# A graph layer on one core: a small first block of dst, another order of additions and one-hots, banks shared out anew, and earlier x work

## The chip, the cores and the metric

The kernel runs on one core of one Trainium2 chip. The metric is the device time of one execution in microseconds; a median of several runs is compared.

TensorE multiplies and accumulates into PSUM, VectorE does elementwise work and reductions, ScalarE applies functions and copies, GpSimd clears memory and issues a few transfers, and the sync engine (SP) only issues transfers. Each engine takes its instructions in the order in which the program gives them to it.

## The reference

There are N = 12500 nodes with 128 features (x) and E = 412500 edges with 48 features. dst holds each edge's receiving node and is sorted. With one graph, whose 64 global numbers are u:

```python
h   = maximum(layernorm(x), 0)                          # [N, 128]
agg = segment_sum(edge_attr, dst, num_segments=N)       # [N, 48]
z   = relu(concat([h, agg, u]) @ W1 + b1)               # W1 [240, 256]
out = x + z @ W2 + b2                                   # W2 [256, 128]
```

All of it is float32.

## The kernel before, in words

**Sums over edges.** A chunk is 768 edges, 128 partitions with T = 6 edges each; there are 538 chunks. CG = 6 chunks make a group. The edges are swept in two halves at once, s = 0 and s = 1[...]: half 0 sums into partitions 0 to 47 of aggT, half 1 into 64 to 111. aggT is laid out with features on partitions and nodes along the free axis.

As dst is sorted, the edges of a chunk meet a window of 36 nodes. `onehot` (L296, VectorE) compares each edge's shifted dst (`rel`) with 0 to 35. `contract` (L306, TensorE) multiplies the edges (as weights) with these one-hots, six matmuls for a chunk of each half, into a PSUM bank of the group (`acc`). `add` (L322, VectorE) adds the 153 columns of a group's bank into aggT at an address that it reads from `lo_i`. There are NI = 45 groups in each half.

**Shifted dst.** dst comes in blocks of IB = 9 groups of both halves, 108 rows of 768 numbers. `shift_dst` (L345 to L348) makes the base of each row with a small matmul (`brow`, L328) and a ScalarE copy, and subtracts it on VectorE (`df`). `spread` (L361, L362) turns df with TensorE's transposes and copies it to `rel`, in two halves of three.

**The layer.** Nodes are taken in blocks of 512, four to a partition; a pair is one block from the lower and one from the upper half of the nodes, so that the two sweeps complete a pair together. There are 12 pairs and a middle block of 212 nodes. For a pair: `load_x` and `next_x` (L204, ScalarE's queue), `normalization` (statistics L432, variance, L418 to L422, and ReLU on ScalarE, L428), `transpose` (L444, copy L447), `hidden_x` (L462: x part of the first layer, one block and one half of the hidden units; with the first half also xb = x + b2, L458), `hidden_sums` (L473: sums part of both blocks, then ReLU to `hid`, L481), `output` (L492) and `store` (L500, L503). The x tiles have XBUFS = 3 buffers; xb is the last reader of one.

**The order.** It is written out by hand (`manual_schedule`). The main loop goes by steps of one chunk of each half. In each step it emits the contraction, then what stands at that step: at k = 0 and k = 3 of a group the one-hots of one half of the next group, followed by the addition of the group before; then stores that are due; then one part of the normalization (`next_part`); then `pieces` of the layer (transposes, hidden parts, outputs), each with a first step and a price, as far as a credit of 0.56 a step reaches. A pair's pieces become due when both sweeps have passed it (`ready`). A pair's statistics are followed by its ReLU rows, which wait in the list until the pair before has been transposed. As soon as both xb of a pair have been emitted, the load of the pair three further on is put into `x_loads`; `next_x` issues from it at every tenth step, or at once when the normalization gets to that pair. Edge loads go out on SP's queue, each after its buffer was read; PF = 15 buffers of two chunks. dst loads and stores of the output go on the same queue.

PSUM has eight banks here: three for group sums, one for transposes, two for the first layer, two for outputs.

Of the kernel before, what the change touches and what calls it, by code (L numbers as in the profile page):

```python
# [12 lines left out]
OP = mybir.AluOpType  # L13
# [8 lines left out]
def kernel(  # L22
# [50 lines left out]
    NG = -(-E // GE)  # L73
    NI = NG // 2
    IB = 9
    NB = NI // IB
    CB = IB * CG
    assert NG == 2 * NI and NI == NB * IB
# [6 lines left out]
    PF = 15  # L85
# [10 lines left out]
    for k in range(NP):  # L96
# [7 lines left out]
    HIGH = [END - OFF[-1] - W, N - 1]  # L104
    assert LOW[1] + OFF[0] + shift[1] == 0
    NC = max(HIGH[0] + WG, HIGH[1] - LOW[1] + WG, END + PAD + WA)


    ready = [min(NI - 1, max(
        int(-(-(blocks[j][0] + BN + PAD + 1 - LEAST - s * NI * GSTEP) // GSTEP)) - 1  # L110
# [7 lines left out]
    psh = ctx.enter_context(tc.tile_pool(name="ps_h", bufs=2, space=bass.MemoryType.PSUM))  # L118
# [7 lines left out]
    ohp = edge_ctx.enter_context(tc.tile_pool(name="oh", bufs=6))  # L126

    aggT = big.tile([P, NC], F32)
    brow = const.tile([1, NB, 2, IB, CG], F32)
# [8 lines left out]
    def load_edges(e, c0, n):  # L138
# [15 lines left out]
    chunks = [min(CG, NCH - g * CG) for g in range(NG)]  # L154
    edges, hots, rels = {}, {}, {}

    ends = [min(s * NI * CG + NI * CG, NCH) for s in range(2)]
    e_loads = sorted(
        (c - s * NI * CG, s, c, min(CL if c > NI * CG or s == 0 else 1, ends[s] - c))
        for s in range(2) for c in ([] if s == 0 else [NI * CG]) + list(range(s * NI * CG + s, ends[s], CL)))  # L160
# [9 lines left out]
    def load_chunks(di, at, c, n):  # L170

        full = max(0, min(n, NFULL - c))
        nc.sync.dma_start(di[at:at + full], dst[c * CE:(c + full) * CE].rearrange("(c e) -> c e", e=CE))
        if full < n:
            for q in range(0, CE, TAIL):
                m = min(TAIL, CE - q)
                nc.sync.dma_start(di[at + full:at + n, q:q + m], dst[None, E - m:E])

    rows_in = [CB + sum(chunks[NI + b * IB:NI + (b + 1) * IB]) for b in range(NB)]

    def load_dst(b):
        di = dp.tile([P, CE], I32, name="di", bufs=2)
        for s in range(2):
            g = s * NI + b * IB
            load_chunks(di, s * CB, g * CG, sum(chunks[g:g + IB]))
        return di
# [30 lines left out]
    mids = [min(g * GE + GE // 2, E - 1) for g in range(NG)]  # L217
    nf = min(sum(m == g * GE + GE // 2 for g, m in enumerate(mids)), E // GE)
# [8 lines left out]
    with nc.allow_non_contiguous_dma(reason="a few hundred numbers, once"):  # L227
        nc.sync.dma_start(first[:, :nf], dst[:nf * GE].rearrange("(a g e) -> a g e", a=1, e=GE)[:, :, GE // 2])
        for g in range(nf, NG):
            nc.sync.dma_start(first[:, g:g + 1], dst[None, mids[g]:mids[g] + 1])  # L230
        dis = {0: load_dst(0)}
        for i in range(PF):
            next_edges()
# [6 lines left out]
    for s in range(2):  # L240
        nc.gpsimd.memset(low[:, s * NI:(s + 1) * NI], float(LOW[s]))
        nc.gpsimd.memset(high[:, s * NI:(s + 1) * NI], float(HIGH[s]))
# [12 lines left out]
    cut = NC * 5 // 8  # L255
    for c in range(0, cut, 1024):
        nc.gpsimd.memset(aggT[:, c:min(c + 1024, cut)], 0.0)
# [4 lines left out]
    nc.gpsimd.iota(least, pattern=[[1, NG]], base=0, channel_multiplier=0,  # L262
# [18 lines left out]
    for i in range(3):  # L281
        ps = psum.tile([P, 512], F32, name=f"ps{i}")
        nc.scalar.copy(ps, zero.to_broadcast([P, 512]))
        acc.append(ps)
    nc.scalar.copy(aggT[:, cut:], zero.to_broadcast([P, NC - cut]))


    def onehot(s, i, k0=0, k1=CG):
        if i < NI:
            g = s * NI + i  # L290
            n = min(k1, chunks[g]) - k0
            if k0 == 0:
                hots[g] = ohp.tile([P, CG * T, W], F32, name="oh")
            c = s * CB + i % IB * CG + k0
            r = rels[i // IB][:, c:c + n, :].rearrange("p c t -> p (c t)")
# [3 lines left out]
    def contract(i, k):  # L299
# [3 lines left out]
        groups = [(s, s * NI + i) for s in range(2) if k < chunks[s * NI + i]]  # L303
        for t in range(T):
            for s, g in groups:
                nc.tensor.matmul(  # L306
                    ps[s * HI:s * HI + DE, o:o + W], edges[g * CG + k][0][:, t * DE:(t + 1) * DE],
                    hots[g][:, k * T + t, :], start=(k == 0 and t == 0),
                    stop=(k == chunks[g] - 1 and t == T - 1), skip_group_check=True)
        for s, g in groups:  # L310
            if edges.pop(g * CG + k)[1]:
                next_edges()

    def add(s, i):
# [3 lines left out]
            lo_i[0:1, g:g + 1], engines=[DVE], min_val=0, max_val=HIGH[s] - LOW[s],  # L318
# [6 lines left out]
    def first_nodes():  # L325

        for s in range(2):
            nc.vector.tensor_tensor(  # L328
                brow[:, :, s].rearrange("a b i k -> a b (i k)").rearrange("a b (i k) -> a b i k", k=CG),
                offs[:, None, None, :].to_broadcast([1, NB, IB, CG]),  # L330
                first[:, s * NI:(s + 1) * NI].rearrange("a (b i) -> a b i", i=IB)[:, :, :, None]
                .to_broadcast([1, NB, IB, CG]), OP.add)
# [8 lines left out]
    def shift_dst(b, di):  # L341
# [3 lines left out]
        nc.tensor.matmul(pb[:rows], brow[:, b].rearrange("a s i k -> a (s i k)")[:, :rows], one, start=True, stop=True)  # L345
# [5 lines left out]
    def spread(b, df, rows, parts=(0, 1), start=False):  # L351

        dv = df.rearrange("c (p t) -> c t p", t=T)
        if 0 in parts:
            rels[b] = dp.tile([P, P, T], F32, name="rel", bufs=2)
        q = T // 2
        for t0 in [a * q for a in parts]:
            own = start and t0
            pt = (psh if own else pst).tile([P, q, P], F32, name="ph" if own else "pt")
            for t in range(q):  # L360
                nc.tensor.transpose(pt[:, t, :rows], dv[:rows, t0 + t, :], ident[:rows, :rows])  # L361
            (nc.vector.tensor_copy if own else nc.scalar.copy)(  # L362
                rels[b][:, :rows, t0:t0 + q].rearrange("p c t -> p t c"), pt[:, :, :rows])
# [9 lines left out]
    def decide():  # L373
# [4 lines left out]
        nc.vector.tensor_scalar(least, least, GSTEP, float(LEAST), OP.mult, OP.add)  # L378
# [60 lines left out]
    def transpose(j):  # L439
# [6 lines left out]
        hT = mp.tile([P, P, R], F32, name="hT", bufs=3)  # L446
# [5 lines left out]
    def hidden_x(k, a, j):  # L452
# [7 lines left out]
        phs[j] = psh.tile([P, BN], F32, name="ph")  # L460
        for c in (0, HI):
            nc.tensor.matmul(phs[j][c:c + HI, :R * m], w1h[:, a * P + c:a * P + c + HI], hTs[j][:, :R * m],  # L462
                             start=True, stop=False, skip_group_check=True)

    def hidden_sums(k, a):

        js = pairs[k]
        if len(js) == 2:
            for s, j in enumerate(js):
                at = blocks[j][0] + shift[s]  # L470
                h = slice(s * HI, s * HI + DE)
                for c in (0, HI):
                    nc.tensor.matmul(phs[j][c:c + HI], w1a[h, a * P + c:a * P + c + HI], aggT[h, at:at + BN],  # L473
                                     start=False, stop=True, skip_group_check=True)
        else:
            for c in (0, HI):
                nc.tensor.matmul(phs[js[0]][c:c + HI, :NM], w1a[:K2, a * P + c:a * P + c + HI], mid[:K2],
                                 start=False, stop=True, skip_group_check=True)
        for j in js:
            m = blocks[j][1]  # L480
            nc.scalar.activation(hids[j][:, a, :, :m], phs.pop(j)[:, :R * m].rearrange("h (p r) -> h r p", r=R),  # L481
# [35 lines left out]
    pieces = [(18, 0.9, lambda: turn(0)), (20, 0.9, lambda: turn(1))]  # L517
    for k, js in enumerate(pairs):
        at = CG * ((ready + [NI - 1])[k] + 1) + 4
        nxt = pairs[k + 1] if k + 1 < len(pairs) else []  # L520
        if len(js) == 1:
            pieces.append((at, 0.0, lambda: copy_middle(0)))
        for a in range(NH):
            for j in js:
                pieces.append((at - 2, 0.9, lambda k=k, a=a, j=j: hidden_x(k, a, j)))
            pieces.append((at, 0.9, lambda k=k, a=a: hidden_sums(k, a)))
# [12 lines left out]
    def next_part(force=False):  # L539

        nonlocal begun
        if not parts and begun < len(pairs):
# [30 lines left out]
    first_nodes()  # L573
    dfs = {0: shift_dst(0, dis[0])}
    spread(0, dfs[0], rows_in[0], start=True)
    for k0 in (0, CG // 2):
        for s in range(2):
            onehot(s, 0, k0, k0 + CG // 2)
    first_columns()
    next_x()  # L580
    next_x()

# [151 lines left out]
```

## Time and profile before

| | |
|---|---|
| runs | 362.89, 357.94, 361.99 us; median 361.99 |
| profiled execution | 365.58 us; its span 363.5 |
| mean TensorE clock in it | 0.946 |
| TensorE busy | 315.6 us (87%), 7785 instructions |
| VectorE busy | 230.0 us (63%) |
| ScalarE busy | 110.6 us (30%) |
| moved | 95.37 MB, 262 GB/s over the span |
| edge matmuls, L306 | 195.0 us busy, 25.3 us idle before them |
| one-hots, L296 | 134.1 us busy, 1461 ns of one |

The span runs from the first to the last instruction. A busy time is the sum of an engine's instructions; for TensorE their ends are modelled. "Idle before" is how long the engine stood still ahead of instructions of that group, and the name behind it is what ended the wait; "issue" means that the profile shows nothing that it waited for. The clock is the share of full speed that TensorE was granted. The first edge matmul starts at 10.91 us and the last ones end near 327.5 us; the last instruction of TensorE ends at 356.4 us.

### The profile page before, as it was taken

The page shows a single profiled execution, that of the slowest core. Times are in us where ns is not written, and L with a number is a line of the kernel's source. Part 1 is how long each engine was busy: PE and PEld are TensorE (multiplying, and loading weights), DVE is VectorE, ACT ScalarE, POOL GpSimd, SP SyncE. Part 2 cuts the span into 40 slices and gives each one's busy share as a digit, 9 for nine tenths or more (in the row PEclk, how much of TensorE's full clock was granted, in tenths as well). Part 3 has the DMA queues.
Part 4 walks back from the last instruction along what each step waited for, and adds up shares of the span by engine and source line. Part 5 has one row for each costly group of instructions (what it writes and reads, how often), then busy time and mean ns, then how long its engine had stood idle before and what let it go on. Part 6 is the DMA issues. An engine that isn't in the chain of part 4 may idle for free.

```text
span 363.5 us, 17319 instructions
## 1 busy us (share of the span) xinstructions
PE 315.6 (87%) x7785; PEld 252.4 (69%) x7786; DVE 230.0 (63%) x445; ACT 110.6 (30%) x231; POOL 10.8 (3%) x40
## 2 busy tenths in 40 slices
PE   1788599999969989988999998999899979998781
PEld 1777576866956877766886885886696766884271
DVE  1877698577566577756578587569458566833220
ACT  6105042325212341521251263033243241243230
POOL 9200000000000000000000000000000000000000
PEclk9969989999998999999899999699899998999987
DMA  6999999999996999999799949999889997510101
GB/s 178 334 334 347 359 359 330 307 324 345 307 286 189 309 303 289 318 313 301 207 304 316 300 136 351 358 303 326 273 271 313 299 320 221 163 62 2 58 35 46
DMA packets 81233, 95.37 MB, mean 262 GB/s; under 512 B 5484, under 2 KB 74234, under 8 KB 81149
## 3 DMA queue, kind: packets, MB, share of 16 engines
q1 hardware_dynamic: 77331, 87.27, 76.0%
q10 hardware_dynamic: 3530, 6.40, 5.2%
q8 instruction: 63, 1.03, 1.2%
q0 software_dynamic: 288, 0.49, 0.5%
q14 instruction: 21, 0.17, 0.1%
HBM read 87.75 MB, written 6.40 MB: 259 GB/s over the span
## 4 chain that ended last, share of the span: by engine, by line
PE 80%; DMA 6%; issue 6%; DVE 4%; ACT 1%; SPq 1%; DVEq 0%; ACTq 0%
PE ps L306 42%; PE po L492 13%; PE ph L462 11%; PE ph L473 7%; PE pt L444 4%; DMA e<-in_edge_attr_dram 3%; DVE oh L296 2%; DMA xt<-in_x_dram 2%; PE pt L361 1%; DMA di<-in_dst_dram 1%; ACT hid L481 1%; DVE aggT L322 0%; ACT xn L428 0%; DVE df L348 0%; DVE xb L458 0%
## 5 line engine op out<-in xcount | busy, mean ns | idle before, releaser
L306 PEld LDWEIGHTS ps<-oh,e 128*48 128x48 f32 x6456 | 186.0, 131 | 75.2 <-issue 68.3
L306 PE MATMUL ps<-oh,e 128*48 128x36 f32 x6456 | 195.0, 218 | 25.3 <-issue 21.7
L296 DVE TENSOR_TENSOR oh<-iota,rel 128x1296 f32<-128x1296 f32 (+1 forms) x92 | 134.1, 1461 | 0.3
L481 ACT ACTIVATE hid<-ph,bias 128x512 f32<-128x512 f32 (+1 forms) x50 | 31.3, 675 | 127.1 <-PE ph L473 121.4
L492 PE MATMUL po<-w,hid 128*64 128x128 f32 (+1 forms) x784 | 64.6, 290 | 0.2 <-ACT hid L481 0.2
L462 PE MATMUL ph<-hT,w1h 128*64 128x512 f32 (+1 forms) x200 | 52.9, 606 | 1.5 <-ACT hid L481 1.5
L322 DVE TENSOR_TENSOR aggT<-aggT,ps 48x153 f32 x90 | 28.0, 311 | 40.4 <-PE ps L306 28.2
L500 DVE TENSOR_TENSOR ot<-po,xb 128x512 f32<-128x512 f32 (+1 forms) x25 | 17.3, 691 | 50.4 <-PE po L492 50.1
L492 PEld LDWEIGHTS po<-w,hid 128*64 128x64 f32 (+1 forms) x784 | 45.7, 144 | 1.2 <-ACT hid L481 0.8
L428 ACT ACTIVATE xn<-xt,sh,sc 128x128 f32<-128x128 f32 (+1 forms) x100 | 40.5, 483 | 3.1 <-DVE sh L422 2.3
L447 ACT COPY hT<-pt 128x512 f32<-128x512 f32 (+1 forms) x25 | 14.4, 576 | 55.3 <-PE pt L444 54.9
L473 PE MATMUL ph<-aggT,w1a 48*64 48x512 f32 x192 | 27.3, 631 | 4.1 <-DVE aggT L322 4.1
L432 DVE BATCH_NORM_STATS2 st<-xt 128x6 f32<-128x128 f32 (+1 forms) x100 | 23.6, 279 | 8.7 <-DMA xt<-in_x_dram 8.3
L444 PE MATMUL pt<-ident,xn 128*128 128x128 f32 (+1 forms) x100 | 17.9, 298 | 2.3 <-ACT xn L428 1.7
L458 DVE TENSOR_TENSOR xb<-xt,b_sb 128x512 f32<-128x512 f32 (+1 forms) x25 | 16.8, 683 | 0.2
L444 PEld LDWEIGHTS pt<-ident,xn 128*128 128x128 f32 (+1 forms) x100 | 11.2, 146 | 5.8 <-ACT xn L428 3.6
L462 PEld LDWEIGHTS ph<-hT,w1h 128*64 128x64 f32 x200 | 11.4, 140 | 5.4 <-ACT hid L481 4.1
L362 ACT COPY rel<-pt 128x324 f32<-128x324 f32 (+1 forms) x9 | 6.8, 754 | 23.4 <-PE pt L361 21.4
L348 DVE TENSOR_TENSOR df<-di,base 108x768 f32<-108x768 int32 (+1 forms) x5 | 4.8, 955 | 13.3 <-ACT base L346 6.7
L370 ACT ACTIVATE far<-df,bounds 108x768 f32<-108x768 f32 (+1 forms) x10 | 9.4, 936 | 7.4 <-DMA e<-in_edge_attr_dram 7.3
L473 PEld LDWEIGHTS ph<-aggT,w1a 48*64 48x64 f32 x192 | 5.2, 131 | 7.9 <-DVE aggT L322 4.5
L146 POOL MEMSET e<- 128x288 f32 x1 | 0.3, 343 | 299.9 <-PE ps L306 299.9
(74 smaller groups left out, 63.8 us busy)
## 6 DMA issues: line engine op xcount, KB each, us to landing
e<-in_edge_attr_dram SPq DMA_DIRECT2D x268, 288.0 KB
xt<-in_x_dram ACTq DMA_DIRECT2D x24, 256.0 KB
out_dram<-ot SPq DMA_DIRECT2D x24, 256.0 KB
di<-in_dst_dram SPq DMA_DIRECT2D x9, 162.0 KB
di<-in_dst_dram SPq DMA_DIRECT2D x1, 153.0 KB
e<-in_edge_attr_dram SPq DMA_DIRECT2D x1, 144.0 KB
di<-in_dst_dram SPq DMA_DIRECT2D x9, 0.3 KB
w1h<-in_L_gnn_W_dram POOLq DMA_DIRECT2D x1, 128.0 KB, 6.6
```

The costliest lines, as they stand in the source:

```text
L296: nc.vector.tensor_tensor(hots[g][:, k0 * T:(k0 + n) * T], iota[:, None, :].to_broadcast([P, n * T, W]), r[:, :, None].to_broadcast([P, n ...
L306: nc.tensor.matmul(ps[s * HI:s * HI + DE, o:o + W], edges[g * CG + k][0][:, t * DE:(t + 1) * DE], hots[g][:, k * T + t, :], start=(k == 0 ...
L322: nc.vector.tensor_tensor(to, to, acc[i % len(acc)][h, :wg], OP.add)
L428: nc.scalar.activation(xns[j][:m, r], xs[j][:m, r], AF.Relu, bias=sh[:m, c:c + 1], scale=sc[:m, c:c + 1])
L432: parts.append((k, None, lambda i=i, j=j, r=r: nc.vector.bn_stats(st[:m, i * R + r, :], xs[j][:m, r, :])))
L444: nc.tensor.transpose(pt[:, r, :m], xn[:m, r], ident[:m, :m])
L458: nc.vector.tensor_tensor(xb[:m], xs[j][:m], b2_sb[:m, None, :].to_broadcast([m, R, D]), OP.add)
L462: nc.tensor.matmul(phs[j][c:c + HI, :R * m], w1h[:, a * P + c:a * P + c + HI], hTs[j][:, :R * m], start=True, stop=False, skip_group_check ...
L473: nc.tensor.matmul(phs[j][c:c + HI], w1a[h, a * P + c:a * P + c + HI], aggT[h, at:at + BN], start=False, stop=True, skip_group_check=True)
L481: nc.scalar.activation(hids[j][:, a, :, :m], phs.pop(j)[:, :R * m].rearrange("h (p r) -> h r p", r=R), AF.Relu, bias=bias[:, a:a + 1])
L492: nc.tensor.matmul(pos[j][c:k, r], hids[j][:, a, r, c:k], w2[:, a], start=(a == 0), stop=(a == NH - 1), skip_group_check=True)
L500: nc.vector.tensor_tensor(ot[:m], pos.pop(j)[:m], xbs.pop(j)[:m], OP.add)
```

## The change

- **Blocks of dst.** Blocks begin at groups 0, 2, 11, 20, 29 and 38, so the first holds two groups of each half (24 rows). The halves are split at chunk 269 (`C0`), so the last group of both halves is short. The first block's dst goes on ScalarE's queue and the second's on SP's behind the seventh edge load. `rel` is one tile for each half, so `spread` copies twice.
- **VectorE's order.** Both additions of the group before stand at k = 0, ahead of the next group's one-hots; one-hots of half 0 follow at k = 0, of half 1 at k = 2. One-hot tiles have two buffers for each half instead of six in all. The very first one-hots come in thirds.
- **PSUM.** Three banks for the first layer, two for group sums.
- **Layer.** The first two pairs are transposed from steps 8, 11, 14 and 17. Later, pairs are transposed two ahead instead of one (hT has four buffers), x parts are due eight steps before the sums instead of two, and one x part of the second half stands ahead of the first sums. Parts of the normalization come two in a step in the first 20 steps and in odd steps later; a pair is begun only when its x buffer can have been freed. Credit is 0.54 a step, up to 1.2. `next_x` stands at steps 4, 7, 12 and then every eighth.
- **Others.** PF is 18. GpSimd clears all of aggT. The loop ends three steps after the last contraction.

```diff
-    PF = 15
+    PF = 18
...
-    psh = ctx.enter_context(tc.tile_pool(name="ps_h", bufs=2, space=bass.MemoryType.PSUM))
+    psh = ctx.enter_context(tc.tile_pool(name="ps_h", bufs=3, space=bass.MemoryType.PSUM))
...
-    ohp = edge_ctx.enter_context(tc.tile_pool(name="oh", bufs=6))
+    ohp = edge_ctx.enter_context(tc.tile_pool(name="oh", bufs=2))
...
-    for i in range(3):
+    for i in range(2):
         ps = psum.tile([P, 512], F32, name=f"ps{i}")
...
-    pieces = [(18, 0.9, lambda: turn(0)), (20, 0.9, lambda: turn(1))]
+    order = [j for js in pairs for j in js]
+    pieces = [(8 + 3 * j, 0.9, lambda j=j: turn(j)) for j in order[:4]]
     for k, js in enumerate(pairs):
-        at = CG * ((ready + [NI - 1])[k] + 1) + 4
-        nxt = pairs[k + 1] if k + 1 < len(pairs) else []
+        at = CG * ((ready + [NI - 1])[k] + 1) + 2
+        nxt = pairs[k + 2] if k + 2 < len(pairs) else []
...
-        for a in range(NH):
-            for j in js:
-                pieces.append((at - 2, 0.9, lambda k=k, a=a, j=j: hidden_x(k, a, j)))
-            pieces.append((at, 0.9, lambda k=k, a=a: hidden_sums(k, a)))
+        parts_of = [(at - 8, 0.9, lambda k=k, a=a, j=j: hidden_x(k, a, j)) for a in range(NH) for j in js]
+        sums = [(at, 0.9, lambda k=k, a=a: hidden_sums(k, a)) for a in range(NH)]
+        m = len(js)
+        pieces += parts_of[:m + 1] + sums[:1] + parts_of[m + 1:] + sums[1:]
...
-        if not parts and begun < len(pairs):
+        if not parts and begun < min(len(pairs), freed + XBUFS):
             normalization(begun)
...
+    for step in [4, 7] + list(range(12, CG * NI, 8)):
+        at_step(0, step, next_x)
...
-        if k in (0, 3):
-            onehot(k // 3, i + 1)
-            if 0 <= i - 1 < NI:
-                add(k // 3, i - 1)
+        if k == 0:
+            if i > 0:
+                add(0, i - 1)
+                add(1, i - 1)
+        if k == 0:
+            onehot(0, i + 1)
+        if k == 2:
+            onehot(1, i + 1)
         store_late()
-        if step >= 4:
+        for _ in range(2 if step % 2 or step < 20 else 1):
             next_part()
-        if step >= 14 and step % 10 == 4:
-            next_x()
-        credit = min(credit + 0.56, 1.0)
+        credit = min(credit + 0.54, 1.2)
```

## The prediction

> **What bounds the kernel now.** I read the page's summary first, then the chain, the waits of the sync engine's DMA queue by stretch, and the order of time where TensorE stops.
>
> ```profile
> span 363.5 us, 17319 instructions
> PE 315.6 (87%) x7785; PEld 252.4 (69%) x7786; DVE 230.0 (63%) x445; ACT 110.6 (30%) x231; POOL 10.8 (3%) x40
> PE 80%; DMA 6%; issue 6%; DVE 4%; ACT 1%; SPq 1%; DVEq 0%; ACTq 0%
> ```
>
> TensorE is the bound: 80% of the chain. The DMA engines look full, but the sync queue waits for landings only early. The waits of 30 to 60 us (first line) and of 60 to 100 us (the other two; us, times, longest):
>
> ```profile
> SPq L142 <- DMA e<-in_edge_attr_dram: 10.6, 17, 2.7
> ...
> SPq L142 <- PE ps L306: 16.9, 23, 1.7
> SPq L142 <- DMA e<-in_edge_attr_dram: 2.5, 2, 1.7
> ```
>
> From 60 us edge loads wait for buffers that TensorE frees, so a TensorE stall is lost time. It also costs twice, as pairs of stretches show, a gap and what follows (stretch, its us, busy us of TensorE, weight loads, VectorE, ScalarE, GpSimd, then TensorE's clock, DMA share, GB/s):
>
> ```profile
> 19.00:20.60 1.60, 0.05 (x3) 0.02 (x2) 0.00 (x0) 0.00 (x0) 0.00 (x0) 1.00 1.09 368
> 20.60:27.00 6.40, 6.36 (x129) 6.13 (x131) 6.34 (x14) 0.00 (x0) 0.00 (x0) 0.50 1.08 330
> 107.00:109.10 2.10, 0.05 (x2) 0.00 (x0) 2.07 (x4) 0.00 (x0) 0.00 (x0) 1.00 1.05 343
> 109.10:114.00 4.90, 4.85 (x74) 2.70 (x76) 4.40 (x9) 1.27 (x2) 0.00 (x0) 0.65 0.40 122
> 226.20:227.80 1.60, 0.04 (x1) 0.00 (x0) 0.19 (x2) 0.56 (x2) 0.00 (x0) 1.00 1.08 372
> 227.80:236.00 8.20, 8.19 (x142) 7.88 (x143) 4.50 (x7) 0.74 (x2) 0.00 (x0) 0.58 1.09 357
> ```
>
> These gaps are followed by clocks of 0.50, 0.65, 0.58: 3.2, 1.7, 3.4 us lost. Of ten gaps of 1.4 us or more seven had such a sequel, about 2 us each; three had none.
>
> VectorE's order is the other thing to see. In time order:
>
> ```profile
> 13.28 3.23 ACTq L204 DMA_DIRECT2D xt<-in_x_dram  x2
> 20.61 0.49 DVE L432 BATCH_NORM_STATS2 st<-xt 128x6 f32<-128x128 f32 x2 [3.54 <-DMA xt<-in_x_dram]
> 21.02 1.49 DVE L296 TENSOR_TENSOR oh<-iota,rel 128x1296 f32<-128x1296 f32 x1
> ...
> 109.15 1.84 PE L473 MATMUL ph<-aggT,w1a 48*64 48x512 f32 x8 [2.10 <-DVE aggT L322]
> 345.92 1.42 PE L444 MATMUL pt<-ident,xn 53*128 53x53 f32 x4 [1.73 <-ACT xn L428]
> ```
>
> Statistics that wait for x hold back the one-hots queued behind them (3.54 us). TensorE at L473 waits for VectorE's latest addition into aggT. The last line is a stall of the tail.
>
> **What the Trainium skill says.** "TensorE: Matmul & The Clock Gate", Part 1: the default clock is half speed, and idle windows of about 3.4 us bring it back. The trace agrees on the half (0.50), but gaps of 1.6 us were enough. "DMA: Bandwidth & Descriptors", Anatomy of one DMA: about 2.0 us fixed plus bytes over 436 GB/s (a software-queue fit), an estimate of 2.6 us for 256 KB. The chain of waits has one x load from 181.45 to 184.23, 2.78 us; in the saturated start one took 5.52. I use 2.8. "Perfetto Trace Analysis", Per-engine timelines: VectorE's queue is strictly first in, first out; the lines at 20.61 and 21.02 agree.
>
> **Part by part.** Durations: one step of edge matmuls 0.58 us (48 loads in 1.16), hidden_x 0.95, hidden_sums 1.02, one-hots 1.5, an addition 0.32, xb 0.65, statistics 0.25.
>
> *Start.* Edge matmuls run steadily from 11.66. The small block drops the 2.21 us clearing of aggT from ScalarE's path, shrinks brow (2 of 0.42) and the rel copies (0.72; 36 columns instead of 324), and one-hots come in thirds (1.5 times 432/1296, 0.5). df stays 0.96 (768 columns for 24 rows too). From the landing of first at 3.4: brow 0.3, matmul and copy to base (ScalarE is free near 4.7) 1.0, df 0.96 and its 0.1 of waits, transposes 0.8, rel 0.5, two one-hot thirds 1.0: a start near 8.5, a gain of 3. It is given back: statistics of pair 0, then df of block 1, stand ahead of the one-hots of group 1, and x still lands near 15. Following both queues, group 1 starts near 18.5, group 2 near 27 (24.8 before), group 4 near 42.3; at 42.3 the old kernel is 5.5 steps further (3.2 us), but the new one has done 2.8 us of transposes ahead. Net 0, from -3 to +4. The new dst loads keep their bytes; block 1's load on SP holds eleven edge loads for 0.33 MB, 1 us, in a full queue. GpSimd's longer clearing (seven instructions for four of 0.95 us) starts its weight loads 2.5 us later; step 10 is their first user, hidden; otherwise at most 2.5. The split rel copies (two for one of 0.75) lie in ScalarE's 70% of idle time; up to 0.5 per half block, ten of them, if not. Ten tiny loads at the tail of dst held SP for 8.1 us near 206 and still do, earlier by 10 steps; three more edge buffers hide them, else 1.6 (the gap at 226.2).
>
> *Additions first, two banks, two one-hot buffers.* hidden_sums no longer finds additions behind one-hots: the waits of 2.1 and 1.6 us (near 109 and 172) go, with their slow clocks (4.9 and 4.8 us at 0.65, 1.7 each): -7. Next late is VectorE: additions 0.65 and two one-hots 3.0 fit into a group's 3.5 us of edge matmuls only barely, with hidden_x (2.85) easily. Behind the addition's wait for the previous group stand both one-hots of the next.
>
> *Statistics now run to the limit of the x buffers.* This is the costly part. Before, next_x ran 5 to 15 steps ahead of a pair's statistics. Now parts run a pair further ahead with XBUFS still 3, so pair k+3's load is issued just after the last xb of pair k frees its buffer, and its statistics stand next on VectorE, ahead of additions. For k=2, from the end of group 11: additions 0.65, one-hots 1.5, xb 0.65, one-hots 1.5, xb 0.65: 4.95. Load 2.8, its second half 0.75 later: 8.5; statistics and additions 1.1: 9.6. TensorE needs six steps and three hidden_x, 6.35, then three steps, 1.75: at 8.1 it stands at hidden_sums, which reads aggT: a stall of 1.5. Pair 6 (k=3): df of block 3 stands between the one-hots, after TensorE's base matmul at 2.7, so xb ends at 6.2, additions at 10.8; sums come one step into the next group, at 7.2: 3.6. Pair 7 (k=4): the second one-hots stand behind two statistics, 2.8 + 2.8 + 0.5 + 1.5 = 7.7 against 6.4 of TensorE, and once more a group later, 0.9: 2.2. Pair 3 starts with VectorE late (one-hots of group 4 at 42.3): 3.0. Pairs 4, 8, 9, 10, 11, 12 by their own orders: 1.4, 1.3, 2.0, 2.2, 2.0, 3.0. With 1.5 for pair 5 the ten sum to 22 us. Ten gaps times 0.7 times 2 us of slow clock add 14. Some old "issue" gaps (1.4 to 2.7 us, in mid-step) will hide in these: -5. Net +31; from 0 (landings within 1.3 us) to 58 (5.5 us, ten times 2.7 more).
>
> *Tail.* From 327.5 to 356.4 TensorE does two pairs and the middle. Now one pair and the middle remain: four hidden_x 3.8, two sums 2.0, two waits for hid 1.6 (0.8 each, as at 329.76), outputs 5.1, middle 4.0: 16.5. Moved into the loop: two hidden_x, two sums, three transposes (0.6), 32 output matmuls (3.95): 9.7. Net 28.9 - 16.5 - 9.7 = -2.7; with three banks and the last transposes early, between -5 and 0.
>
> Sum: 0 - 7 + 31 - 2.7 = +21.3 on the profiled execution's 365.6, 387. That execution is 1% above the median of the runs, 361.99; with the difference carried over: 383.
>
> **Rivals.** *The wait is absorbed* (faster). VectorE is idle 37% of the time; if x lands soon enough that additions are done when TensorE reaches hidden_sums (point of decision: 1.3 us after issue, or TensorE later by that much), only -7 and -2.7 stay, and -3 of the start: 349 to 352. For it: VectorE is 2 to 4 us ahead of TensorE in many places. Against: 2.78 measured, and load issue hangs on VectorE itself. *The stalls replace the old ones* (no change): the mid-loop issue gaps, some 13 us with 8 of slow clock, vanish while TensorE waits elsewhere: 383 - 21 = 362. *Saturated landings* (worse): 5.5 us instead of 2.8: 383 + 27 = 410; against it, edge loads stop queueing at 60 us. That x parts come early may also do nothing: credit, not their due step, mostly sets them; that is within the tail's bounds.
>
> **How the numbers follow.** Forecast 0.58, worse 0.05, no change 0.13, faster 0.24. The forecast's own range is 371 to 396 (clock sequels between none and all, the start's bounds). To leave out at most 2 in 10, the range goes down to 351, halfway into the faster case, and up to 396. About 2% is what a measurement of this kernel tells from no change. Slower 0.62, same 0.14, faster 0.24.
>
> **What would show it.** Waits of VectorE's statistics for x of 2 to 4 us, ten times; waits of TensorE's sums and edge matmuls for VectorE of 15 to 25 us in all; a mean clock below 0.946; first edge matmul before 9.5; TensorE's work after the last edge matmul near 17 us. I'm wrong if statistics hardly wait for x, or if TensorE's waits for VectorE stay below 8 us.

## The result and the profile after

The changed kernel takes 422.8 us (median of 4 runs, 421.2 to 426.1), the kernel before 362.4 us in the same comparison: a ratio of 1.173 with a 95% interval of 1.159 to 1.186. The direction was forecast, the size was not: 383 us was predicted, and 396 us was the upper end of the range. The profiled execution took 426.1 us, its span is 424.1 us.

Lines have moved in the changed kernel: contract is L321, onehot L311, add L337, statistics L459, hidden_x L489 (xb L485), hidden_sums L500, output L519, df L366, the copies to rel L379 and L380, the x load L211.

The page's summary and the first line of its chain, kernel after:

```profile
span 424.1 us, 17390 instructions
PE 339.3 (80%) x7793; PEld 263.1 (62%) x7794; DVE 234.0 (55%) x460; ACT 111.1 (26%) x247; POOL 13.0 (3%) x44
PE 54%; DMA 18%; DVE 18%; issue 4%; ACT 2%; DVEq 1%; SPq 1%; ACTq 0%
```

TensorE has fallen from 80% of the chain to 54%; DMA and VectorE have 18% each. Two sums say where the 60.6 us of span went. TensorE's idle time (span less busy time) rose from 363.5 - 315.6 = 47.9 to 424.1 - 339.3 = 84.8 us: 36.9 us. Its busy time rose by 23.7 us for nearly the same instructions (7785 before, 7793 now). That second part goes with the clock, whose mean fell from 0.946 to 0.878.

The waits of the engines, kernel after (us in total, times, longest):

```profile
DVE st L459 <- DMA xt<-in_x_dram: 68.1, 14, 7.2
PE ph L500 <- DVE aggT L337: 34.1, 8, 6.5
PE ps L321 <- DVE oh L311: 12.7, 5, 5.5
PE ph L500 <- issue: 7.1, 1, 7.1
PE ps L321 <- issue: 3.6, 8, 0.8
```

VectorE's statistics wait for x for 68.1 us; before it was 8.3 us in 3 waits. TensorE's sums wait 34.1 us for additions, its edge matmuls 12.7 us for one-hots; before, 4.1 and 3.2. The edge matmuls' issue gaps have shrunk from 21.7 to 3.6 us.

One of the ten waits in time order, kernel after (start, duration, engine, line, what; in brackets the idle time before it and what ended it):

```profile
123.77 0.68 DVE L485 TENSOR_TENSOR xb<-xt,b_sb 128x512 f32<-128x512 f32 x1
...
124.46 2.32 PE L321 MATMUL ps<-oh,e 128*48 128x36 f32 x96
...
124.48 0.82 ACTq L211 DMA_DIRECT2D xt<-in_x_dram  x2
129.88 1.29 DVE L459 BATCH_NORM_STATS2 st<-xt 128x6 f32<-128x128 f32 x5 [5.43 <-DMA xt<-in_x_dram]
131.48 0.31 DVE L337 TENSOR_TENSOR aggT<-aggT,ps 48x153 f32 x1 [0.31 <-DVE st L459]
...
131.84 2.54 PE L500 MATMUL ph<-aggT,w1a 48*64 48x512 f32 x8 [5.06 <-DVE aggT L337]
...
134.31 2.14 PE L321 MATMUL ps<-oh,e 128*48 128x36 f32 x48
```

The last xb of a pair frees the x buffer, ScalarE issues both loads at once, and the next instruction of VectorE needs them. The additions stand behind the statistics, and TensorE, done with its edge matmuls at 126.78, stands at the sums until 131.84.

The same place in stretches, kernel after (stretch, its us, busy us of TensorE, weight loads, VectorE, ScalarE, GpSimd, then TensorE's clock, DMA share, GB/s):

```profile
127.00:129.00 2.00, 0.00 (x0) 0.00 (x0) 0.00 (x0) 0.00 (x0) 0.00 (x0) 1.00 1.07 370
129.20:131.80 2.60, 0.00 (x0) 0.00 (x0) 1.48 (x6) 0.00 (x0) 0.00 (x0) 0.59 1.08 360
131.80:146.00 14.20, 13.24 (x168) 8.15 (x168) 8.23 (x17) 2.72 (x5) 0.00 (x0) 0.50 0.52 152
146.50:150.00 3.50, 3.50 (x110) 3.50 (x108) 0.30 (x1) 2.44 (x5) 0.00 (x0) 0.97 0.77 208
```

The clock falls while TensorE is still idle, and stays at half for 14 us after it has resumed: half of 13.2 busy us, 6.6, are lost after a gap of 5. After the gaps of 1.6 us shown of the kernel before it was 3.2 to 3.4.

### The profile page after: what moved, and what is told of

It reads as the page before. It is cut to its first block, busy times and chain, and to the rows that moved or that the text cites. A ratio compares the mean times of both kernels' runs of the same rounds, so it can differ in the third digit from the quotient of the medians.

```text
span 424.1 us, 17390 instructions
## 1 busy us (share of the span) xinstructions
PE 339.3 (80%) x7793; PEld 263.1 (62%) x7794; DVE 234.0 (55%) x460; ACT 111.1 (26%) x247; POOL 13.0 (3%) x44
## 4 chain that ended last, share of the span: by engine, by line
PE 54%; DMA 18%; DVE 18%; issue 4%; ACT 2%; DVEq 1%; SPq 1%; ACTq 0%
PE ps L321 26%; DMA xt<-in_x_dram 13%; PE po L519 11%; DVE oh L311 9%; PE ph L500 7%; PE ph L489 6%; DMA e<-in_edge_attr_dram 5%; PE pt L471 4%; DVE xb L485 2%; DVE aggT L337 2%; DVE st L459 2%; ACT xn L455 1%; ACT hid L508 1%; PE pt L387 1%; DVE ot L527 1%
## 5 line engine op out<-in xcount | busy, mean ns | idle before, releaser
L321 PEld LDWEIGHTS ps<-oh,e 128*48 128x48 f32 x6456 | 191.0, 137 | 78.2 <-issue 63.9
L321 PE MATMUL ps<-oh,e 128*48 128x36 f32 x6456 | 197.7, 223 | 16.5 <-DVE oh L311 12.7
L311 DVE TENSOR_TENSOR oh<-iota,rel 128x1296 f32<-128x1296 f32 (+2 forms) x94 | 133.8, 1440 | 4.7 <-ACT rel L379 3.5
L500 PE MATMUL ph<-aggT,w1a 48*64 48x512 f32 x192 | 38.6, 772 | 41.2 <-DVE aggT L337 34.1
L337 DVE TENSOR_TENSOR aggT<-aggT,ps 48x153 f32 (+1 forms) x90 | 28.0, 311 | 75.9 <-PE ps L321 61.5
L489 PE MATMUL ph<-hT,w1h 128*64 128x512 f32 (+1 forms) x200 | 60.7, 686 | 1.9 <-ACT hid L508 1.9
L459 DVE BATCH_NORM_STATS2 st<-xt 128x6 f32<-128x128 f32 (+1 forms) x100 | 22.6, 280 | 68.2 <-DMA xt<-in_x_dram 68.1
L519 PE MATMUL po<-w,hid 128*64 128x128 f32 (+1 forms) x784 | 57.7, 278 | 0.7 <-ACT hid L508 0.7
L519 PEld LDWEIGHTS po<-w,hid 128*64 128x64 f32 (+1 forms) x784 | 42.5, 137 | 2.6 <-ACT hid L508 1.4
L500 PEld LDWEIGHTS ph<-aggT,w1a 48*64 48x64 f32 x192 | 8.4, 154 | 47.2 <-DVE aggT L337 37.5
L474 ACT COPY hT<-pt 128x512 f32<-128x512 f32 (+1 forms) x25 | 14.4, 575 | 47.1 <-PE pt L471 47.1
L445 ACT ACTIVATE sc<-va,eps 128x8 f32<-128x8 f32 (+1 forms) x13 | 3.9, 301 | 84.5 <-DVE va L444 81.2
L471 PE MATMUL pt<-ident,xn 128*128 128x128 f32 (+1 forms) x100 | 18.8, 314 | 4.4 <-ACT xn L455 3.4
L485 DVE TENSOR_TENSOR xb<-xt,b_sb 128x512 f32<-128x512 f32 (+1 forms) x25 | 16.8, 683 | 0.0
L489 PEld LDWEIGHTS ph<-hT,w1h 128*64 128x64 f32 x200 | 12.6, 154 | 4.6 <-ACT hid L508 3.2
L387 PE MATMUL pt<-ident,df 108*128 108x108 f32 (+2 forms) x33 | 7.6, 347 | 8.2 <-DVE df L366 8.2
L379 ACT COPY rel<-pt 128x162 f32<-128x162 f32 (+2 forms) x11 | 4.6, 415 | 29.7 <-PE pt L387 29.7
```

The source lines that it names most:

```text
L311: nc.vector.tensor_tensor(hots[g][:, k0 * T:(k0 + n) * T], iota[:, None, :].to_broadcast([P, n * T, W]), r[:, :, None].to_broadcast([P, n ...
L321: nc.tensor.matmul(ps[s * HI:s * HI + DE, o:o + W], edges[c][0][:, t * DE:(t + 1) * DE], hots[g][:, k * T + t, :], start=(k == 0 and t == ...
L337: nc.vector.tensor_tensor(to, to, acc[i % len(acc)][h, :wg], OP.add)
L459: parts.append((k, None, lambda i=i, j=j, r=r: nc.vector.bn_stats(st[:m, i * R + r, :], xs[j][:m, r, :])))
L471: nc.tensor.transpose(pt[:, r, :m], xn[:m, r], ident[:m, :m])
L485: nc.vector.tensor_tensor(xb[:m], xs[j][:m], b2_sb[:m, None, :].to_broadcast([m, R, D]), OP.add)
```

## The experiments

The theory (A): VectorE stands still at statistics whose x could be issued only when VectorE itself had freed the buffer, and TensorE pays with idle time and with the slow clock. The rivals: the order and the fewer banks leave no slack whatever x does (B); what makes x land late is the larger number of edge loads (C) or the pair's two loads together (D).

The readings of the runs that bear on x, in one table. "x waits" are those of VectorE's statistics, "sums" the waits of TensorE's sums for additions, "idle" is TensorE's (span less busy), all of the profiled execution, which isn't the median run (e13's took 373.6 us, the kernel before's 365.6); a dash means below 2 us. e1, e3, e4, e5, e6 and e9 were run once.

| | time, us | x waits | sums | TensorE busy | idle |
|---|---|---|---|---|---|
| before | 362.4 | 8.3 | 4.1 | 315.6 | 47.9 |
| after | 422.8 | 68.1 | 34.1 | 339.3 | 84.8 |
| e1, after, statistics of a resident tile | 351.4 | none | - | 308.7 | 40.6 |
| e2, after, pair begun one later | 360.6 | 9.0 | - | 310.8 | 47.9 |
| e3, before, x issued late in the program | 369.7 | 20.0 | 13.1 | 313.2 | 54.4 |
| e4, after, nine edge buffers | 423.5 | 65.5 | 33.7 | 336.0 | 85.5 |
| e5, before, two x buffers | 388.2 | 59.3 | 18.1 | 323.9 | 62.3 |
| e6, after, one block of x | 416.3 | 65.0 | 29.9 | 334.0 | 80.4 |
| e7, after, four x buffers | 353.6 | 9.1 | - | 310.0 | 40.7 |
| e9, after, half the edge bytes | 397.2 | 43.2 | 22.0 | 337.1 | 57.9 |
| e13, after, statistics behind additions | 370.0 | 32.2 | 4.9 | 324.4 | 47.1 |

**Is it the wait for x? (e1, e2, e7)**

e1:

```diff
-    nc.vector.bn_stats(st[:m, i * R + r, :], xs[j][:m, r, :])
+    nc.vector.bn_stats(st[:m, i * R + r, :], ident[:m])
```

> The changed kernel, whose statistics read the resident identity tile instead of xt: the true mean and variance are left out, everything else and the order of every queue stay. Theory A (VectorE's queue stands still at statistics whose x was issued just before, and TensorE pays with idle time and with the slow clock after it): VectorE's waits for x, 68 us, go; TensorE's busy time falls from 339 to about 316 us, the clock rises to 0.94 or more, and the time is 345 to 360 us. Theory B (two group banks, two one-hot buffers for each half and a denser order leave TensorE without slack against VectorE, whatever x does): TensorE's waits for VectorE stay above 40 us and the time is over 395 us.

Measured 351.4 us, clock 0.988. With every queue in the same order, 71 us vanish with this one dependence.

e2:

```diff
-        if not parts and begun < min(len(pairs), freed + XBUFS):
+        if not parts and begun < min(len(pairs), freed + XBUFS - 1):
```

> The changed kernel, where a pair is begun one pair later; the three x buffers and all else stay, so that x loads go out 11 to 24 steps ahead of the statistics. Theory A: statistics wait for x only in the start, under 15 us in all; 345 to 360 us, faster than the kernel before. Theory B: over 395 us. If half of the loss is in the other parts: near 385 us.

Measured 360.6 us, a ratio to before of 1.004 (1.000 to 1.007). The waits for x went as expected, but 9 us of the gain are missing. The waits name them, kernel e2:

```profile
PEld pt L471 <- ACT xn L455: 12.5, 15, 5.4
PE pt L471 <- ACT xn L455: 9.2, 6, 5.3
```

The transposes now wait for normalized rows, since a pair that is begun later is ready later. So the early statistics are wanted; what they lacked was x.

e7:

```diff
-    XBUFS = 3
+    XBUFS = 4
...
-        if not parts and begun < min(len(pairs), freed + XBUFS):
+        if not parts and begun < min(len(pairs), freed + 3):
```

> The changed kernel with four x buffers and the same limit on beginning a pair: x loads go out 10 to 24 steps ahead of the statistics, which keep their early place. Theory A: the same as with statistics that read a resident tile, 349 to 355 us, statistics waiting for x only in the start. If the early statistics themselves (and not the missing lead) crowd VectorE: 360 us or more, as with the pair begun later.

Measured 353.6 us, a ratio to before of 0.978 (0.971 to 0.986), about 2% faster than the kernel before: of the versions that compute the whole result, the fastest. Its page and its waits, in two fences:

```profile
span 350.7 us, 17389 instructions
PE 310.0 (88%) x7793; PEld 246.4 (70%) x7794; DVE 232.8 (66%) x460; ACT 110.9 (32%) x247; POOL 13.1 (4%) x44
```

```profile
DVE st L459 <- DMA xt<-in_x_dram: 9.1, 2, 7.2
```

Two waits are left, both in the start. Theory A is shown, and B is refuted as a cause of its own: the same two banks, the same one-hot buffers and the same order run in 353.6 us. Against e7 the changed kernel has 44.1 us more of idle and 29.3 us more of busy TensorE, 73.4 us, which together are the difference of the two spans.

**What makes x late? (e4, e6, e9)**

e4:

```diff
-    PF = 18
+    PF = 9
```

> The changed kernel with PF 9 instead of 18 edge buffers, half as many edge loads that can stand ahead of x. Theory C (x lands after 5 to 6.5 us and not 2.8 because it shares the DMA engines with a backlog of edge loads that the larger PF allows): landing of the first block of a pair near 3 to 4 us, VectorE's waits for x down from 68 to 45 us or less, 385 to 405 us. Theory D (the pair's two loads, 512 KB together instead of 256, and edges that TensorE eats faster than they can land fill the DMA engines with nine buffers as well): landing still 5 to 6 us, waits for x 60 to 70 us, 415 to 435 us.

Measured 423.5 us, landings of 5 to 7 us on the chain from 80 us on: the number of edge buffers isn't it. C falls in this form. The traces give a likely reason. A transfer reports its end to a semaphore (a counter), most with sixteen signals, and in this program all transfers of SP's and ScalarE's queues use eight semaphores in turn. Each is issued only after the one before it on its semaphore has landed: in the traces of e4 and of the changed kernel never more than eight are under way at once, with nine edge buffers or with eighteen.

e6:

```diff
-            xs[j] = xt[:, i].rearrange("p (r d) -> p r d", d=D)
-            x_loads.append((k, lambda i=i, j=j: load(i, j)))
+            xs[j] = xt[:, 0].rearrange("p (r d) -> p r d", d=D)
+            if i == 0:
+                x_loads.append((k, lambda i=i, j=j: load(i, j)))
```

> The changed kernel, where only the first block of each pair is loaded and the second block's statistics, rows and xb read it too: the second block's x is left out, 256 KB instead of 512 KB for a pair. If x lands late because the pair's two loads share the engines (5.4 us for the first, 6.0 for the second): landing 3 to 4 us, VectorE's waits for x 68 us down to 30 to 45, 380 to 400 us. If a backlog of edge loads makes it late: landing 5 to 6 us, waits above 55 us, 410 to 425 us.

Measured 416.3 us, waits still 65.0 us, landings of 4.9 to 6.4 us: half of x hardly lands sooner. D falls. What the DMA engines did in the wait at 124.48 shows why. The queues in two stretches, kernel after (packets, MB, share of 16 engines); the first line is of 124.5 to 127.0 us, the other two of 127.5 to 129.0:

```profile
q1 hardware_dynamic: 864, 0.97, 108.1%
...
q10 hardware_dynamic: 207, 0.39, 72.4%
q1 hardware_dynamic: 139, 0.14, 28.8%
```

q10 is ScalarE's queue, which carries x; q1 is SP's, which carries the edges. For 2.5 us after the issue not one packet of x moves, though q1's packets fill all engines; then x has most of them. About 1 MB of edge packets goes first, three to four loads of 288 KB, which nine buffers hold as well as eighteen. This is the longest such pause of the ten; in the others the first packet of x comes 1.2 to 2.4 us after the issue, and another 0.6 to 1.3 MB of edges moves while x does.

e9:

```diff
-            load_edges(e, c, n)
+            load_edges(e, c, 1)
             for k in range(n):
-                edges[c + k] = (e[:, k], k == n - 1)
+                edges[c + k] = (e[:, 0], k == n - 1)
```

> The changed kernel, where each edge load brings only the first of its two chunks and the matmuls of the second read the first's: half of the edges is left out of the sums, the instructions of every engine stay. If x lands late because its packets stand behind edge packets already handed to the DMA engines: landing near 3 us instead of 5.5 to 6.5, VectorE's waits for x 68 us down to 25 to 40, and with them the size that the prediction took: 380 to 395 us. If the landing is the load's own time: waits above 55 us, 410 us or more.

Measured 397.2 us, 2 us beyond the expected band; landings of 2.9 to 4.4 us on the chain from 80 us on, waits down to 43.2, 3 us above their band. The queues in e9 after an issue at 149.62 (first line: 149.60 to 150.55 us, the others: 150.60 to 151.50):

```profile
q1 hardware_dynamic: 94, 0.10, 51.5%
...
q10 hardware_dynamic: 103, 0.21, 80.2%
q1 hardware_dynamic: 44, 0.04, 11.8%
```

The edge traffic ahead of x and beside it makes it late, then. About 1.0 us without a packet of x stays even here, where the edges take only half of the engines, so by an estimate from these two about 1.5 of the 2.5 us above are the edges'. The run shows a second thing: with waits a third shorter, idle time fell by 26.9 us, but busy time only from 339.3 to 337.1. The slow clock costs 27 us above e7 here, nearly as much as with the long waits.

**What makes the wait so dear? (e3, e5, e13)**

e3:

```diff
-        if step >= 14 and step % 10 == 4:
-            next_x()
```

> The kernel before, with the regular next_x at every tenth step taken out: x of a pair is issued right ahead of its statistics, as in the changed kernel, and nothing else of the change is in it. Theory A: the order alone is enough; some twelve waits of 4.5 to 6 us at the statistics, TensorE idle 25 to 40 us more, clock below 0.91, 400 to 425 us. Theory B: three group banks and six one-hot buffers take up most of it; 365 to 380 us.

Measured 369.7 us with only four waits, 20.0 us. The time lies in B's band, but it doesn't speak for B, since the edit hardly made the wait: the loads stand late in the program, but their buffers were free long before, and ScalarE reaches them ahead of VectorE (for one pair, issued at 106.52, statistics at 113.03). A late place in the program alone doesn't make the wait, then. e5 frees the buffer just ahead:

```diff
-    XBUFS = 3
+    XBUFS = 2
...
-        if not parts and begun < len(pairs):
+        if not parts and begun < min(len(pairs), freed + XBUFS):
```

> The kernel before with two x buffers and the changed kernel's limit (a pair is begun only when its buffer can have been freed), so that a pair's loads wait for the last xb of the pair two back and its statistics stand two to five steps behind that; the statistics keep their place. Theory A (the load hangs on a buffer that VectorE's own queue frees just ahead, in any order of the rest): about ten waits of VectorE for x of 2 to 5 us, TensorE idle 10 to 25 us more than before, 378 to 405 us. Theory B (the old order with three group banks has the slack): the same waits, but TensorE idle less than 8 us more, 362 to 372 us.

Measured 388.2 us (before on the same chip 361.0), within A's band, with 14 waits of 59.3 us: a buffer that VectorE frees just ahead makes the wait in the old order too. But 51.0 us more of waiting cost 27.2 us, 0.53 us for each, where the changed kernel pays (422.8 - 353.6) / (68.1 - 9.1) = 1.17. So B holds in part: it isn't a cause, but the old order takes more than half of the same wait. The likely place was the sums, which wait 34.1 us for additions in the changed kernel and 18.1 in e5. e13 puts the changed kernel's additions ahead of the statistics, with three x buffers:

```diff
-        if not parts and begun < min(len(pairs), freed + XBUFS):
+        if not parts and begun < min(len(pairs), freed + XBUFS) and (
+                force or begun < 3 or step % CG == 0):
```

> The changed kernel with its three x buffers, where a pair (from the fourth on) is begun only at k = 0 of a group, so that both additions and one one-hot tile stand ahead of the statistics on VectorE; the loads still hang on the last xb. VectorE's waits for x should fall by the 2.15 us of those instructions a pair, 68 us to about 45. If TensorE pays 1.17 us for each us of VectorE's wait above the 9 us of the run with four x buffers (353.6), as in the changed kernel: 353.6 + 36 x 1.17 = 396 us. If the dear part is that the sums wait for an addition that stands behind the waiting statistics: TensorE's waits at the sums fall from 34 us to under 10, each us costs 0.5 as in the kernel before with two x buffers, 372 us.

Measured 370.0 us, a ratio to before of 1.025 (1.014 to 1.036). The waits of e13 and of the changed kernel differ most in the sums:

```profile
DVE st L459 <- DMA xt<-in_x_dram: 32.2, 11, 6.4
...
PE ph L500 <- DVE aggT L337: 4.9, 4, 1.6
```

VectorE's waits fell further than expected (a later beginning also gives x some lead), but the price fell too: 16.4 us for 23.1 us of waits above e7, 0.71 each. That takes the time from the median and the waits from the profiled execution, the slowest of four. The spans of the profiled executions alone give (371.5 - 350.7) / 23.1 = 0.90, where the changed kernel has 73.4 / 59.0 = 1.24. That 370 comes so near the 372 expected is thus luck in part: there were fewer waits than was assumed, and each cost more. e9 is the control, with shortened waits and the additions still behind: each us cost (397.2 - 353.6) / (43.2 - 9.1) = 1.28 (1.30 by the spans), and its sums wait 22.0 us. So a part of the price lies in sums that wait for an addition behind the waiting statistics. How much exactly stays open, since e13's waits are also shorter one by one (mostly 2.0 to 2.6 us, for 3 to 4 in e9), and what else separates 0.71 to 0.90 from the old order's 0.53 wasn't taken apart. Of the 20.8 us of span above e7, TensorE's idle time is only 6.4; the other 14.4 are busy time, the slow clock that still follows e13's shorter gaps.

**Additions first by themselves (e10, e11)**

e10, the kernel before:

```diff
-            onehot(k // 3, i + 1)
             if 0 <= i - 1 < NI:
                 add(k // 3, i - 1)
+            onehot(k // 3, i + 1)
```

> The kernel before, with each addition issued ahead of the one-hots of its half-group instead of behind them; nothing else. By the prediction's step (the two waits of the sums for the latest addition, 2.1 and 1.6 us, go with 3.4 us of slow clock behind them): 7 us less, a ratio of 0.975 to 0.985. By its rival (VectorE then waits in the addition for the group's matmuls, and the one-hots behind it come late for TensorE): within 1% of before or slower.

Measured 355.3 us, a ratio of 0.985 (0.977 to 0.992), which is 5.6 us off 362. The gain is small beside the spread: the kernel before has a median of 360.0 us on that chip, with single runs from 352.7 to 363.9. TensorE's waits for VectorE, kernel e10:

```profile
PE ps L306 <- DVE oh L296: 9.7, 6, 2.3
PE ph L473 <- DVE aggT L322: 0.6, 2, 0.4
```

The waits of the sums are gone (4.1 us before), and in part the rival's effect is there too: edge matmuls wait 9.7 us for one-hots, for 3.2 before.

e11, four x buffers and additions last:

```diff
-        if k == 0:
-            if i > 0:
-                add(0, i - 1)
-                add(1, i - 1)
         if k == 0:
             onehot(0, i + 1)
         if k == 2:
             onehot(1, i + 1)
+            if i > 0:
+                add(0, i - 1)
+                add(1, i - 1)
```

> The changed kernel with four x buffers, and both additions of a group behind the second one-hots of the next (k = 2) instead of ahead of the first. If additions first are worth 7 us in this order too: near 360 us, a ratio near 1.0 against before, where four x buffers alone had 0.978. If two group banks make late additions dearer than that (TensorE waits for the bank): 365 us or more. If they are worth nothing: 352 to 355 us.

Measured 367.3 us (361.6 to 369.1; before on the same chip 360.0), 14 us above e7. TensorE's sums wait 11.1 us for additions, where e7 has 1.7. Additions first are worth 5 to 6 us in the old order and about 14 in the new one. The time lies in the band named for edge matmuls that wait for a bank, but such a wait shows nowhere in e11.

**The start (e8, e12)**

e8, four x buffers:

```diff
+    next_x()
+    next_x()
     first_nodes(0)
...
     first_nodes(1)
-    next_x()
-    next_x()
```

> As with four x buffers, and x of pair 0 issued ahead of the first copy to base on ScalarE's queue instead of behind the copies to rel: it lands near 12 us instead of 18.9. If the wait of 7 us at the first statistics is what holds up groups 1 and 2: 343 to 348 us. If TensorE in the start is held by edges and one-hots (VectorE) anyway, or x takes the edges' bandwidth: within 2 us of the run with four x buffers.

Measured 357.1 us, a ratio to before of 0.993 (0.989 to 0.998): worse than e7, outside both bands. In time order, kernel e8:

```profile
9.08 1.96 ACTq L211 DMA_DIRECT2D xt<-in_x_dram  x2
11.08 0.15 ACT L364 COPY base<-pt 24x1 f32<-24x1 f32 x1 [6.75 <-DMA e<-in_edge_attr_dram]
11.26 0.95 DVE L366 TENSOR_TENSOR df<-di,base 24x768 f32<-24x768 int32 x1 [7.26 <-ACT base L364]
```

x could be issued only at 9.08, and the two loads held the copy to base behind them on ScalarE until 11.08 (4.35 in e7). What held x is the program's use of semaphores: its first load shares one with the third edge load, whose last signal comes at 9.06. The first edge matmul came at 14.4 instead of 7.6 us.

e12, four x buffers, normalization begun later:

```diff
-        for _ in range(2 if step % 2 or step < 20 else 1):
+        for _ in range(0 if step < 6 else 2 if step % 2 or step < 20 else 1):
             next_part()
...
-    pieces = [(8 + 3 * j, 0.9, lambda j=j: turn(j)) for j in order[:4]]
+    pieces = [(12 + 3 * j, 0.9, lambda j=j: turn(j)) for j in order[:4]]
```

> As with four x buffers, and normalization begun at step 6 instead of step 0 with the first four transposes due four steps later, so that df and the one-hots of group 1 stand ahead of the first statistics on VectorE. If the wait of 7.2 us at the first statistics costs TensorE time that it doesn't get back: 346 to 351 us, a ratio of 0.96 to 0.972. If the start is held by edges and one-hots anyway: the same as with four x buffers, 0.978.

Measured 359.4 us, a ratio of 1.012 (1.007 to 1.017); the medians of all runs, 359.4 and 360.0 us, give 0.998. By either it is slower than e7 with its 0.978. Group 1 starts at 18.8 us instead of 22.5, but group 4 at 52.9 instead of 48.4: VectorE's waits for x fell to 3.3 us, and the first transposes then waited for normalized rows, 11.0 us of TensorE before 60 us. Removing the early wait in this way only moved it.

## Why the prediction was right and wrong

**Statistics up to the limit of the x buffers (+31): right in mechanism, too small, and this is the step that failed.** Waits of VectorE at ten pairs, then additions, then the sums on TensorE: all were found. Two terms of the sum were mis-sized.

The first is the landing. "Load 2.8, its second half 0.75 later" was 5.4 and 6.0 us. The 2.8 was taken from one wait that the trace of before puts down to x. Its neighbourhood, kernel before, in time order:

```profile
181.45 0.34 ACTq L204 DMA_DIRECT2D xt<-in_x_dram  x1
...
183.53 0.66 PE L361 MATMUL pt<-ident,df 108*128 108x108 f32 x3
...
184.22 0.75 ACT L362 COPY rel<-pt 128x324 f32<-128x324 f32 x1 [2.03 <-DMA xt<-in_x_dram]
```

The copy at 184.22 reads transposes that end at 183.53 + 0.66 = 184.19. It waited for these, not for x, which it doesn't read. The queues of before between 184.3 and 185.0 us still carry x:

```profile
q10 hardware_dynamic: 16, 0.02, 7.4%
```

So the load had not landed by then. In the trace its sixteen signals run from 184.23 to 185.03: 2.8 us is the first of them, and the whole load took 3.6. Nor was this load typical. By their last signals the 17 full x loads that the kernel before issues after 60 us took 2.9 to 6.2 us, with a median of 4.5, which could have been read from that trace before. In the changed kernel, from 80 us on, the first load of a full pair takes 4.9 to 6.3 us and the second 5.6 to 7.4. The 5.52 us at 36.11 us, which the prediction set aside as the saturated start, was the better number; "edge loads stop queueing at 60 us" was the wrong reason for it, since a burst of edge matmuls frees buffers and refills the engines at any time (share 1.07, 370 GB/s, at 127 us). e9, with landings of 2.9 to 4.4 us, shows about what the step's working was worth: its idle time is 17.2 us above e7's, where the prediction had 22 of stalls less 5 of old gaps. The longer landing accounts for the other 44.1 - 17.2 = 27 us.

The second is the slow clock. "Ten gaps times 0.7 times 2 us", 14, was 29.3 us against e7, 3 us a pair. The 2 us were those of gaps near 1.6 us. Each of the ten pairs had a gap, one of 2.6 us and nine of 4.4 to 7.1, and the clock stood at half for 3.4 to 17.1 us at each (for 14 us after 131.8). The Trainium skill's "TensorE: Matmul & The Clock Gate", Part 1, whose idle window of 3.4 us the prediction quoted against the shorter gaps, fits these gaps only roughly. The clock of 0.59 on average in the last 2.6 us of the idle time, from 129.2, means half clock from about 129.7, 2.9 us after TensorE stopped, and the gap of 2.6 us brought it too.

In numbers: 15 more of clock and 27 more of idle make 42. The prediction's sum for the profiled execution was 387; 387 + 42 = 429, where 426.1 was profiled. The 3 us between are within the bounds of the other terms.

**Additions first (-7): right in mechanism, a little too large.** It is 5 to 6 us by itself (e10), and the waits of 2.1 and 1.6 us at the sums are gone, in e10 and in e7 (1.7 us in 3 waits).

**Tail (-2.7): right in its length.** Kernel after, in time order, the last edge matmuls and TensorE's last instructions:

```profile
400.73 0.70 PE L321 MATMUL ps<-oh,e 128*48 128x36 f32 x24
...
414.74 2.06 PE L519 MATMUL po<-w,hid 128*53 128x128 f32 x16 [0.25 <-ACT hid L508]
```

From 401.4 to 416.8 it is 15.4 us, for 16.5 predicted. What the work moved into the loop costs there wasn't measured by itself. Together the two gains were put at 9.7 us; e7 and before differ by 7.4 us on the same chip, with a start that is some 6 us later than forecast (group 4 at 48.4 us in e7), so that this agreement is luck in part.

**Start (0, -3 to +4): not quite.** The first edge matmul came at 7.7 (8.5 predicted), but, by a count of the edge matmuls in the trace, 144 to a group, group 1 at 22.4 (18.5), group 2 at 33.8 (27) and group 4 at 47.8 (42.3). x of pair 0 landed at 18.9, not 15. In e1, without that wait, group 4 starts at 46.0. The 5.5 us against the forecast are thus partly x; the rest wasn't settled. They don't reach the end in full, since e7 has this start too and is 7.4 us below before.

**Rivals.** "Absorbed" (349 to 352) is what happens when x isn't waited for (e1 351.4, e7 353.6), but 5.4 us were never within its 1.3. "The stalls replace the old ones" took place as far as the issue gaps go, which shrank by 18 us, though e7, without the stalls, also has only 11.2 us of them; so the stalls can't be credited with all of it. "Saturated landings" had the right landing at 410 us and lacked the clock. It was given a chance of 0.05, too little beside landings of 2.9 to 6.2 us in the trace of before.

Of what was named to prove it, all showed in kind, the first two beyond their bounds: waits of statistics ten times and more, of 5 to 6 us rather than 2 to 4; TensorE's waits for VectorE, 34.1 + 12.7 us and more, for 15 to 25; a clock below 0.946; a first matmul before 9.5; a tail near 17.

## What to carry to other kernels

Follow a load back to what frees its buffer: if that is the engine that next waits for the load, the whole landing stands in that engine's queue, and one more buffer removes it (69 us here). Before a landing time is taken from a wait, see whether the waiting instruction reads that tile at all, whether the load's last signal had come, and whether other packets were in the engines' way; then look at several loads. Before a load is moved to the head of a queue, see with which earlier transfer it shares a semaphore. Of the waits that can't be removed, keep ahead of them on the queue whatever another engine needs next.

## What the runs showed of the hardware

- A load issued on ScalarE's queue moved no packet for 2.5 us while some 1 MB of edge packets from SP's queue drained at 386 GB/s; halving the edge bytes brought the landing from 4.9 to 6.5 down to 2.9 to 4.4 us, and brought the first packet at 149.62 about 1.0 us after the issue. Halving x or the edge buffers hardly changed the landing. The Trainium skill's "DMA: Bandwidth & Descriptors", Anatomy of one DMA, gave an estimate of 2.6 us for the load alone, from a fit of the software queue. The x load that the changed kernel issues at 40.80, with only 0.06 MB of edges ahead and beside, took 2.8 us; the landings beside full edge traffic are about twice as long.
- A gap of 5 us of TensorE was followed by 14 us at half clock; ten gaps came with 29.3 us more of busy time than e7 has, and with 27.1 us when the waits behind them were a third shorter (e9).
- An x load at the head of ScalarE's queue was issued only at 9.08 us, 0.02 us after the last signal of the edge load with which it shares a semaphore, and held back a copy of 0.15 us that needed no DMA (e8).
